# A four-layer conv/attention kernel: the MLP of layer 0 in blocks of 512 pixels, its inner units in two rounds, a chunk's products in four PSUM banks

## The chip, the cores and the metric

The kernel runs on one core of a Trainium2 chip. A core has a matrix engine (TensorE, PE in the profile; PEld is its loading of weights), two elementwise engines that can read the matrix engine's result memory PSUM (VectorE, DVE; ScalarE, ACT), GpSimd (POOL)[...], and SyncE (SP), which here only issues transfers. [...] The metric is device microseconds of the whole program, the median of several runs.

## The reference, cut to what matters

The input is 2 images of 512 channels and 32 x 32 pixels, all float32. Layer 0 is a deformable attention with a learned position bias, and then a two-layer MLP over channels; layers 1, 2 and 3 are attention layers with group norms. The change concerns the MLP and the seams on its two sides:

```
x = x + out                                   # the attention's output
xn2 = _bn(x, bn2_g, bn2_b)
h1 = gelu(einsum('bchw,oc->bohw', xn2, mlp_w1) + mlp_b1)    # 512 -> 2048 channels
x = x + einsum('bchw,oc->bohw', h1, mlp_w2) + mlp_b2        # 2048 -> 512
```

There are 2 x 1024 = 2048 pixels. Layer 1 begins with a group norm of this x, over groups of 16 channels of one image.

## The kernel before, in words

Everything is laid out with channels on the 128 partitions and pixels along the free dimension: x of an image is `xs[b]`, 4 chunks of 128 channels by 1024 pixels.

**The order of the work.** Python loops write out the order by hand. `layer0` and `layers` stand under `in_order`, so each engine runs its instructions in the order in which the code names them. Tiles and pools add the waits between engines. Loops hand small pieces of other work to the engines at given places by advancing generators (`advance`, `drain`).

**Products by seven.** A matrix product is cut in 2 x 2 blocks and done in seven block products instead of eight (the Winograd form of Strassen's scheme). `lefts` (L149) forms the four sums of the left operand, here the weights, and `rights` (L166) those of the right operand, here pixels; each sum is an operation on VectorE, and one overwrites a block of its operand. The seven products are numbered 1 to 7, and sums of them give the four blocks of the result.

**The MLP** (L1290 to L1394). `BLK = 256` pixels make a block, so a product's right operand has `PX = 128` columns. Of each block, the 2048 inner channels are made in MC = 8 steps, called chunks: a chunk gives 128 inner channels of the upper half and 128 of the lower half, for 256 pixels. `products` (L1296) allocates two banks for it, `pma` and `pmb`, and puts four products of 128 columns in the first and three in the second, in the order 1, 2, 6, 7, 5, 4, 3; each is two matmuls (512 input channels, halved, are two chunks of 128). `first_of` (L1320) copies product 1 to `p` on ScalarE; `combined` (L1306) makes the result in four additions on VectorE, `upper`, `u`, the lower half straight into `hid`, and `upper` again. `activated` applies the GELU to both halves with the bias, in two instructions on ScalarE, one chunk later; after it `form_right2` forms the right operand's sums for this chunk in `hidt`. When the eight chunks are done, layer 2 multiplies with `w2`: two halves of the output columns, seven products of eight matmuls each. It opens with product 1 of both halves, whose last matmul stands at L1382 and waits for the last GELU. `added` (L1329) adds bias and result to x and stores it to `x_d`, from which a fallback that normally does not run would start.

**What runs beside it.** Before layer 2 of a block, `normed_rights` (L180) makes the next block's normalised channels on GpSimd, four instructions, and their four sums on VectorE. In the first block `form2` makes the sums of `w2`, eight VectorE instructions of 1024 elements. From the second image on, the chunks advance `norm`, the group norm of layer 1 for the first image: statistics on VectorE, then four activations on ScalarE that write the normalised channels to the tile `hc`. In the last block the load of layer 1's weights (`qkv1`) takes the place of `w1`, after its last reader.

**Memory.** `bridge` has 8 slots of 1024 numbers per partition and outlives layer 0's pools. Layer 0 uses slots 0 to 5 (`h2p`) and 6 and 7 (part of `h2j`) in turn for sums of its bias network, early also for transposed weights (`nat`). At the end of layer 0, the sums of `w1` go to slots 0 to 5, the normalised channels to slot 6 and their sums to slot 7. `ring`, six tiles of 2048, holds the bias network's first layer; two of the six are tiles of layer 0's own pool. The tile `hc` is allocated apart, in `layers`, in the pool `chan`.

**The seam.** `finish_last` (L733) ends layer 0: it finishes the last bias sums (`third`, L651), takes the softmax of the last heads, and projects. In it `right_sums()` calls `normed_rights(0)`, after the two maximum reductions at L758, and `left_sums` forms the sums of `w1` between the last additions.

Of the kernel before, what the change touches and what calls it, by code (L numbers as in the profile page):

```python
# [12 lines left out]
F32 = mybir.dt.float32  # L13
# [66 lines left out]
def kernel(ctx: ExitStack, tc: tile.TileContext, a: dict, out: bass.AP):  # L80
# [56 lines left out]
    BLK = 256  # L137
# [42 lines left out]
    def normed_rights(blk):  # L180

        b, n = blk * BLK // HW, slice(blk * BLK % HW, blk * BLK % HW + BLK)
        xn = bridge[:, 6, :].rearrange("p (k n) -> p k n", k=CC)
        for cc in range(CC):
            nc.gpsimd.tensor_scalar(
                xn[:, cc, :], xs[b][:, cc, n], s2[:, cc : cc + 1], col("bn2_b", cc), ALU.mult, ALU.add
            )
        right, form = rights(xn, bridge[:, 7, : 3 * CC // 2 * PX].rearrange("p (i k n) -> i p k n", i=3, k=CC // 2))
        form(slice(0, CC // 2))
        return right  # L190

    def layer0(l0, fold_d, t2_b, o2_b):
# [7 lines left out]
        h2p = cycle([bridge[:, k, :] for k in range(6)])  # L200
        h2j = cycle([bridge[:, 6, :], bridge[:, 7, :], *(one.tile([P, HW], F32, name=f"h2j{k}") for k in range(2))])
# [46 lines left out]
        ring = [one.tile([P, 2 * HW], F32, name=f"h1{k}") for k in range(2)]  # L248
# [134 lines left out]
        def table(function):  # L383
            nc.scalar.activation(trial[:, 1:2], trial[:, 0:1], function)
# [348 lines left out]
        def finish_last(sim, eights, fours, right_sums, left_sums):  # L733
# [3 lines left out]
            table(AF.Exp)  # L737
            pts = [zt([P, 4, P], "pt") for _ in range(2)]
# [6 lines left out]
            project_out(pps[0], b, 0, [2])  # L745
            for n in halves:
                nc.scalar.activation(simb[:, n], sim[:, n], AF.Identity, bias=simbias[t])
# [11 lines left out]
            right_sums()  # L759
# [56 lines left out]
        nat = [bridge[:, 2 * j : 2 * j + 2, :].rearrange("p h (k n) -> p (h k) n", k=2) for j in range(3)]  # L816
# [179 lines left out]
        left1, form1 = lefts(w1s, [bridge[:, k : k + 2, :] for k in range(0, 6, 2)])  # L996
        right1 = []

        def left_sums():
# [6 lines left out]
            lambda: right1.extend(normed_rights(0)), left_sums(),  # L1006
# [195 lines left out]
    def layers(f, fold_d, t2_b, o2_b, left1, right1):  # L1202
# [5 lines left out]
        chan = f.enter_context(tc.tile_pool(name="chan", bufs=1))  # L1208
# [9 lines left out]
        def group_norm(x, gname, bname, h, small_psum):  # L1218
# [45 lines left out]
            normed = chan.tile([P, CC, HW], F32, name="hc")  # L1264
# [17 lines left out]
        with ExitStack() as mlp:  # L1282
# [8 lines left out]
            def product(pm, i, left, right, cols):  # L1291
                l, r = left[i - 1], right[i - 1]
                accumulate(pm, [(l[:, k, cols], r[:, k, :]) for k in range(l.shape[1])])

            def products(left, right, cols, some, pms=None):

                if pms is None:
                    pms = [bank(f"pm{i}").rearrange("p (j n) -> p j n", j=4) for i in "ab"]
                a, b = pms
                at = {1: a[:, 0], 2: a[:, 1], 6: a[:, 2], 3: a[:, 3], 4: b[:, 0], 5: b[:, 1], 7: b[:, 2]}  # L1300
                for i in some:
                    product(at[i], i, left, right, cols)
                return pms

            def combined(pms, p1, lower):

                a, b = pms
# [3 lines left out]
                def twice(v):  # L1311
                    return v.unsqueeze(1).to_broadcast([P, 2, PX])

                nc.vector.tensor_tensor(upper, a[:, 1:3], twice(p1), ALU.add)  # L1314
                nc.vector.tensor_tensor(u, b[:, 1:3], twice(upper[:, 1]), ALU.add)
                nc.vector.tensor_tensor(lower, b[:, 0:2], twice(u[:, 1]), ALU.add)
                nc.vector.tensor_tensor(upper[:, 1], a[:, 3], u[:, 0], ALU.add)
                return upper.rearrange("p j n -> p (j n)")

            def first_of(pms):  # L1320
                p1 = two.tile([P, PX], F32, name="p1")
                nc.scalar.copy(p1, pms[0][:, 0])  # L1322
                return p1
# [5 lines left out]
            def added(blk, m, src):  # L1329
                b, at = blk * BLK // HW, blk * BLK % HW  # L1330
                x = xs[b][:, m, at : at + BLK]
                nc.vector.scalar_tensor_tensor(x, src, col("mlp_b2", m), x, ALU.add, ALU.add)
                nc.sync.dma_start(out=x_d[b, m, :, at : at + BLK], in_=x)

# [5 lines left out]
            for blk in range(NBLK):  # L1340
                b = blk * BLK // HW
                hid = one.tile([P, HID // P, BLK], F32, name="hid")
                right2, form_right2 = rights(hid, [one.tile([P, HID // P // 2, PX], F32, name=f"hidt{i}") for i in (1, 2, 4)])

                def activated(c, upper):
                    nc.scalar.activation(hid[:, MC + c, :], hid[:, MC + c, :], AF.Gelu, bias=col("mlp_b1", MC + c))
                    nc.scalar.activation(hid[:, c, :], upper, AF.Gelu, bias=col("mlp_b1", c))

                upper = None
                for c in range(MC + 1):  # L1350
                    if c < MC:
                        pms = products(left1, right1, slice(c * P, (c + 1) * P), (1, 2, 6, 7, 5, 4, 3))
                        p1 = first_of(pms)
                    if c:
                        activated(c - 1, upper)
                    if c < MC:
                        upper = combined(pms, p1, hid[:, MC + c, :].rearrange("p (j n) -> p j n", j=2))
                    if c:
                        form_right2(slice(c - 1, c))
                    if blk == 0 and 4 <= c < MC - 1:  # L1360
                        advance(later[0])
                    if b == 1 and c % 2:
                        advance(norm)
                if blk == 0:
                    drain(chain(*later))
                    nc.vector.tensor_scalar(gb3, vb[:, 2, :], col("gamma3"), None, ALU.mult)
                if blk + 1 < NBLK:
                    right1 = normed_rights(blk + 1)
                else:
# [8 lines left out]
                both = [products(left2, right2, cols[c], ()) for c in range(2)]  # L1378
                for ks in (range(MC - 1), range(MC - 1, MC)):
                    for c in range(2):  # L1380
                        for k in ks:
                            nc.tensor.matmul(  # L1382
                                both[c][0][:, 0],
                                left2[0][:, k, cols[c]],
                                right2[0][:, k, :],
                                start=(k == 0),
                                stop=(k == MC - 1),
                            )
# [732 lines left out]
        def pixels3(x):  # L2121
            t = chan.tile([P, CC, HW], F32, name="hc")
            t = [t[:, i, :].rearrange("p (k n) -> p k n", k=2) for i in range(4)]
# [120 lines left out]
    t2_b, o2_b = [const.tile([P, CC], F32, name=name) for name in ("t2_b", "o2_b")]  # L2244
    bridge_stack = ctx.enter_context(ExitStack())
    bridge = bridge_stack.enter_context(tc.tile_pool(name="bridge", bufs=1, side="right"))
    bridge = bridge.tile([P, 8, HW], F32, name="bridge")
    with ExitStack() as l0:
        left1, right1 = layer0(l0, fold_d, t2_b, o2_b)
    with ExitStack() as fast:  # L2250
        layers(fast, fold_d, t2_b, o2_b, left1, right1)
    bad = nc.values_load(flag[0:1, 0:1], min_val=0, max_val=P)
# [88 lines left out]
```

## Time and profile before

Median of three runs: 3326.72 us (3326.65 to 3328.97).

| | |
|---|---|
| profiled execution | 3326.56 us |
| its span, first to last instruction | 3324.8 us |
| TensorE clock granted | 1.00 |
| TensorE busy | 3311.0 us |
| VectorE busy | 2643.8 us |
| ScalarE busy | 1809.0 us |
| GpSimd busy | 672.8 us |
| from 1999.6 to 2402.6 us (the MLP): TensorE busy | 402.0 us of 403.0 |
| the same stretch: VectorE busy | 214.7 us |
| the same stretch: ScalarE busy | 79.2 us |

How to read it: a row of the profile names line, engine, operation, what is written <- what is read, the shape (partitions x elements) and the count, then the busy time and the mean of one in ns, then the time that the engine sat idle just before and what ended that. Times in a timeline are us from the span's start. Instructions that run on one engine follow each other; those of different engines overlap, so only the time on the chain that ends last makes the program longer. A float32 matmul leaves two records.

### The profile page before, as it was taken

To read this page: it belongs to the slowest core of one execution; us is meant where nothing else is said; L and a number is where in the kernel's file an instruction comes from. 1 tells how busy PE (TensorE), PEld (TensorE's weight loads), DVE (VectorE), ACT (ScalarE), POOL (GpSimd) and SP (SyncE) were. 2 spreads that over 40 slices of the span, in tenths; PEclk is the share of its full clock that TensorE was granted. 3 is DMA by queue.
4 is the path that set the end of the run, shared out by engine and by line. 5 is a ranking of instruction groups with operands and counts; after the bars stand their busy time and mean duration, and the time that the engine had idled before them with its cause. 6 is when DMAs were issued, how large, how long until landed. Compare 5 with 4: busy or idle time off the path is not lost.

```text
span 3324.8 us, 60957 instructions
## 1 busy us (share of the span) xinstructions
PE 3311.0 (100%) x24805; PEld 1599.6 (48%) x24805; DVE 2643.8 (80%) x3027; ACT 1809.0 (54%) x2771; POOL 672.8 (20%) x804
## 2 busy tenths in 40 slices
PE   9999999999999999999999999999999999999999
PEld 4333333333333333333333339999953443687777
DVE  7999999999998799999999976455446466665656
ACT  4866877877876677877877642122126245122221
POOL 1333333333333233333333310000000000000000
PEclk9999999999999999999999999999999999999999
DMA  5787787787787577787787741000100100000111
GB/s 177 164 168 151 159 167 158 160 166 152 160 167 159 107 160 155 159 170 158 163 164 155 160 116 58 14 8 14 52 0 14 26 32 17 7 7 4 29 33 37
DMA packets 143121, 342.87 MB, mean 103 GB/s; under 512 B 37104, under 2 KB 52592, under 8 KB 142064
## 3 DMA queue, kind: packets, MB, share of 16 engines
q0 software_dynamic: 68112, 230.21, 37.1%
q1 hardware_dynamic: 71472, 102.12, 10.1%
q10 hardware_dynamic: 3248, 6.56, 0.5%
q8 instruction: 197, 3.23, 0.4%
q14 instruction: 92, 0.75, 0.1%
HBM read 71.46 MB, written 10.83 MB: 25 GB/s over the span
## 4 chain that ended last, share of the span: by engine, by line
PE 97%; issue 1%; ACT 1%; DVE 1%; POOL 0%; ACTq 0%; DVEq 0%; POOLq 0%
PE z L632 53%; PE pw L1479 6%; PE pma L135 6%; PE pmb L135 5%; PE pmv L1479 4%; PE score L1660 4%; PE pv L1672 3%; PE pm L1479 3%; PE score L1479 3%; PE pmt L1479 1%; PE ppr L1479 1%; PE pp L721 1%; PE sim L661 1%; PE pf L135 1%; PE pma L1382 1%
## 5 line engine op out<-in xcount | busy, mean ns | idle before, releaser
L632 PE MATMUL z<-wa,cpb_w 128*32 128x512 f32 x10880 | 1193.1, 593 | 0.5
L641 ACT ACTIVATE h<-z,b2h 128x1024 f32<-128x1024 f32 x768 | 851.2, 1113 | 327.7 <-PE z L632 316.9
L615 DVE CUSTOM_DVE_ANT_1 wa<-tab,pairs 128x2048 f32<-128x2048 f32 x340 | 779.3, 2293 | 2.7 <-PE z L632 2.4
L632 PEld LDWEIGHTS z<-wa,cpb_w 128*32 128x32 f32 x10880 | 346.1, 110 | 806.0 <-issue 713.5
L632 PE MATMUL z<-h,cpb_w 128*32 128x512 f32 x5504 | 609.4, 593 | 0.3 <-ACT h L641 0.2
L615 DVE CUSTOM_DVE_ANT_1 h<-tab,pairs 128x2048 f32<-128x2048 f32 x172 | 394.4, 2294 | 1.2 <-PE z L632 1.0
L632 PEld LDWEIGHTS z<-h,cpb_w 128*32 128x32 f32 x5504 | 175.4, 110 | 409.5 <-issue 360.1
L646 DVE SCALAR_TENSOR_TENSOR h<-h,turn,h 128x1024 f32<-128x1024 f32 x256 | 329.4, 1287 | 5.5 <-ACT h L641 5.5
L641 ACT ACTIVATE bridge<-z,b2h 128x1024 f32<-128x1024 f32 x162 | 180.6, 1115 | 118.2 <-PE z L632 118.2
L966 POOL DMA_DIRECT2D bridge<-bridge x150 | 127.5, 850 | 532.7 <-DMA bridge<-h 502.3
L646 DVE SCALAR_TENSOR_TENSOR bridge<-bridge,turn,h 128x1024 f32<-128x1024 f32 x162 | 208.1, 1285 | 3.0 <-ACT bridge L641 2.9
L974 POOL DMA_DIRECT2D bridge<-h x160 | 150.3, 939 | 287.3 <-DVE h L646 166.2
L1322 ACT COPY p<-pma 128x128 f32<-128x128 f32 x80 | 21.2, 266 | 335.7 <-PE pma L135 335.7
L1314 DVE TENSOR_TENSOR upper<-pma,p 128x256 f32<-128x256 f32 x80 | 33.8, 422 | 178.9 <-ACT p L1322 178.8
L1661 ACT ACTIVATE p<-score 128x512 f32<-128x512 f32 x256 | 129.7, 628 | 79.8 <-PE score L1660 79.4
L966 POOL DMA_DIRECT2D h2j<-h2j x90 | 76.2, 846 | 312.3 <-DMA h2j<-h 296.7
L1693 DVE TENSOR_TENSOR acc<-acc,p 128x1024 f32<-128x1024 f32 x96 | 111.4, 1219 | 28.4 <-ACT p L1661 28.4
L641 ACT ACTIVATE h2j<-z,b2h 128x1024 f32<-128x1024 f32 x94 | 104.9, 1116 | 42.7 <-PE z L632 42.7
L646 DVE SCALAR_TENSOR_TENSOR h2j<-h2j,turn,h 128x1024 f32<-128x1024 f32 x94 | 121.1, 1288 | 0.2
L1660 PE MATMUL score<-q,k 64*128 64x512 f32 x512 | 119.6, 604 | 0.0
L1672 PE MATMUL pv<-p,vT 128*64 128x512 f32 x512 | 116.5, 598 | 0.0
L979 POOL DMA_DIRECT2D bridge<-bridge x90 | 110.4, 1226 | 1.2 <-DMA bridge<-bridge 0.9
(468 smaller groups left out, 4363.2 us busy)
## 6 DMA issues: line engine op xcount, KB each, us to landing
bridge<-h POOLq DMA_DIRECT2D x160, 512.0 KB, 5.1
h2j<-h POOLq DMA_DIRECT2D x93, 512.0 KB, 5.5
bridge<-bridge POOLq DMA_DIRECT2D x159, 256.0 KB, 3.6
tab<-slog_d SPq DMA_DIRECT2D x128, 256.0 KB, 5.0
h2j<-h2j POOLq DMA_DIRECT2D x90, 256.0 KB, 3.3
bridge<-bridge POOLq DMA_DIRECT2D x150, 128.0 KB, 5.4
bridge<-bridge SPq DMA_DIRECT2D x90, 128.0 KB, 3.7
bridge<-h2j SPq DMA_DIRECT2D x90, 128.0 KB, 3.6
```

Source lines behind the costliest of these rows:

```text
L135: nc.tensor.matmul(pm, w, m, start=(k == 0), stop=(k == len(pairs) - 1))
L615: nc.vector._custom_dve(TENSOR_ADD_SAT, out=h1, in0=tx.unsqueeze(1).to_broadcast([P, H, 2, W]), in1=ty.unsqueeze(3).to_broadcast([P, H, 2, ...
L632: nc.tensor.matmul(z[point * 32 : point * 32 + 32, n], cpb_w2[:, lo : lo + 32], h1s[point][:, half * 16 : half * 16 + 16, :], start=True, ...
L641: nc.scalar.activation(h2, z, AF.Relu, bias=b2h[:, part : part + 1])
L646: nc.vector.scalar_tensor_tensor(h2, h2, turn[:, part // 2 : part // 2 + 1], parts.pop(part + 1), ALU.mult, ALU.add)
L966: nc.gpsimd.dma_start(out=own[0:P:2], in_=own[1:P:2], accum_op=ALU.add)
L974: nc.gpsimd.dma_start(out=joins[i - 1], in_=other, accum_op=ALU.add)
L1479: nc.tensor.matmul(out, stationary(l, k), moving(r, k), start=start and k == 0, stop=k == nk - 1, skip_group_check=not start,)
L1660: nc.tensor.matmul(sc, ks[m][r, s * P : (s + 1) * P], qs[m][r, n], start=True, stop=True)
L1661: nc.scalar.activation(p[:, part], sc, AF.Exp, scale=64 ** -0.5)
L1672: nc.tensor.matmul(pv[half][part * 64 : part * 64 + 64], vt[s % 4][:, lo : lo + 64], lps[s, half][:, part, :], start=(s == 0), stop=(s == 7),)
L1693: nc.vector.tensor_add(acc[half], acc[half], ps[s, half])
```

## The change

`BLK` becomes 512, so a product's right operand has 256 columns. There are 4 blocks in place of 8. So that `hid` does not grow, the inner channels are done in two rounds of RC = 4 chunks each: a round makes half of the inner channels, and its layer 2 adds their part of the output to x. The first round's part comes with the bias; the second round's is added plainly and then stored, so each pixel is stored once. `hid` and its sums are allocated once for all rounds.

A chunk's seven products of 256 columns take four banks (`slots`): 6 and 1, 4 and 5, 7 alone, 3 and 2. They run in the order 1, 6, 7, 5, 4, 2, 3. `combined` now takes the copy of product 1 in, and has six additions: five of 256 elements and one of 512. Layer 2 opens with product 1 of both halves but its last matmul, then product 2 of both halves, then that last matmul.

Normalised channels of a block (2048 numbers now) go to `h1_0`, one of `ring`'s tiles, which moves to the pool of `bridge`; their sums go to two slots of `bridge_b`. `bridge` is cut in `bridge_b` (4 slots) and `hc` (4 slots), allocated before layer 0: layer 0 uses it as slots, the sums of `w1` lie in it during the MLP, and afterwards it holds the normalised channels of the group norms and the sums of layer 3, in place of the tiles of `chan`. So the four activations that write it stand in the last round, after the last product of `w1`. In `finish_last`, the first block's normalised channels are begun at the start and their sums are formed before the maximum reductions.

```diff
-    BLK = 256
+    BLK = 512
     PX = BLK // 2
...
-        xn = bridge[:, 6, :].rearrange("p (k n) -> p k n", k=CC)
+        xn = h1_0.rearrange("p (k n) -> p k n", k=CC)
...
-        right, form = rights(xn, bridge[:, 7, : 3 * CC // 2 * PX].rearrange("p (i k n) -> i p k n", i=3, k=CC // 2))
-        form(slice(0, CC // 2))
-        return right
+        sums = bridge_b[:, 2:4, :].rearrange("p a n -> p (a n)")[:, : 3 * CC // 2 * PX]
+        right, form = rights(xn, sums.rearrange("p (i k n) -> i p k n", i=3, k=CC // 2))
+        return right, lambda: form(slice(0, CC // 2))
...
-        h2p = cycle([bridge[:, k, :] for k in range(6)])
+        h2p = cycle([*(hc[:, k, :] for k in range(4)), *(bridge_b[:, k, :] for k in range(2))])
...
-        ring = [one.tile([P, 2 * HW], F32, name=f"h1{k}") for k in range(2)]
+        ring = [h1_0, one.tile([P, 2 * HW], F32, name="h1_1")]
...
             table(AF.Exp)
+            right_sums()
...
             project_out(pps[0], b, 0, [2])
+            form_right.pop()()
...
-            right_sums()
...
-            normed = chan.tile([P, CC, HW], F32, name="hc")
+            normed = hc
...
+            def slots():
+                some = [bank(f"pm{i}").rearrange("p (j n) -> p j n", j=2) for i in "abcd"]
+                a, b, c, d = some
+                return some, {6: a[:, 0], 1: a[:, 1], 4: b[:, 0], 5: b[:, 1], 7: c[:, 0], 3: d[:, 0], 2: d[:, 1]}
+
+            def product(at, i, left, right, k0, cols, ks, nk):
                 l, r = left[i - 1], right[i - 1]
+                for k in ks:
+                    nc.tensor.matmul(at[i], l[:, k0 + k, cols], r[:, k, :], start=(k == 0), stop=(k == nk - 1))
+
+            def combined(some, at, lower):
...
+                nc.scalar.copy(p1, at[1])
+                nc.vector.tensor_tensor(upper[:, 1], at[6], p1, ALU.add)
+                nc.vector.tensor_tensor(u[:, 1], at[7], upper[:, 1], ALU.add)
+                nc.vector.tensor_tensor(u[:, 0], at[5], upper[:, 1], ALU.add)
+                nc.vector.tensor_tensor(lower, some[1], u[:, 1].unsqueeze(1).to_broadcast([P, 2, PX]), ALU.add)
+                nc.vector.tensor_tensor(upper[:, 0], at[2], p1, ALU.add)
+                nc.vector.tensor_tensor(upper[:, 1], at[3], u[:, 0], ALU.add)
...
-            def added(blk, m, src):
+            def added(blk, m, src, last):
...
-                nc.vector.scalar_tensor_tensor(x, src, col("mlp_b2", m), x, ALU.add, ALU.add)
+                if not last:
+                    nc.vector.scalar_tensor_tensor(x, src, col("mlp_b2", m), x, ALU.add, ALU.add)
+                    return
+                nc.vector.tensor_add(x, x, src)
                 nc.sync.dma_start(out=x_d[b, m, :, at : at + BLK], in_=x)
...
-            for blk in range(NBLK):
+            RC = MC // 2
+            hid = one.tile([P, 2 * RC, BLK], F32, name="hid")
+            hidt = [one.tile([P, RC, PX], F32, name=f"hidt{i}") for i in (1, 2, 4)]
+            for blk, rnd in [(blk, rnd) for blk in range(NBLK) for rnd in range(2)]:
+                last = (blk, rnd) == (NBLK - 1, 1)
+                lo = rnd * RC
...
-                for c in range(MC + 1):
+                for c in range(RC + 1):
...
+                        for i in (1, 6, 7, 5, 4, 2, 3):
+                            product(at, i, left1, right1, 0, slice((lo + c) * P, (lo + c + 1) * P), range(CC // 2), CC // 2)
...
-                    if blk == 0 and 4 <= c < MC - 1:
+                    if blk == rnd == 0 and c == 2:
                         advance(later[0])
-                    if b == 1 and c % 2:
+                    if blk == 2 and c in (1, 2, 3) or blk == 3 and c in (1, 3):
                         advance(norm)
...
+                    drain(norm)
+                elif rnd:
+                    right1, form = normed_rights(blk + 1)
+                    form()
...
+                for i, ks in ((1, range(RC - 1)), (2, range(RC)), (1, range(RC - 1, RC))):
                     for c in range(2):
+                        product(both[c][1], i, left2, right2, lo, cols[c], ks, RC)
                 for c in range(2):
-                    products(left2, right2, cols[c], (2, 6, 7, 5, 4, 3), both[c])
+                    for i in (6, 7, 5, 4, 3):
+                        product(both[c][1], i, left2, right2, lo, cols[c], range(RC), RC)
                     lower = two.tile([P, 2, PX], F32, name="lower")
-                    upper = combined(both[c], first_of(both[c]), lower)
-                    added(blk, 2 + c, lower.rearrange("p j n -> p (j n)"))
-                    added(blk, c, upper)
-        drain(norm)
+                    upper = combined(*both[c], lower)
+                    added(blk, 2 + c, lower.rearrange("p j n -> p (j n)"), rnd)
+                    added(blk, c, upper, rnd)
...
-    bridge = bridge.tile([P, 8, HW], F32, name="bridge")
+    bridge_b = bridge.tile([P, 4, HW], F32, name="bridge_b")
+    h1_0 = bridge.tile([P, 2 * HW], F32, name="h1_0")
```

More of the change, by code (lines that the diff above doesn't have):

```diff
@@ L199, in layer0 @@
         h2q = l0.enter_context(tc.tile_pool(name="att_h2q", bufs=4))
-        h2p = cycle([bridge[:, k, :] for k in range(6)])
-        h2j = cycle([bridge[:, 6, :], bridge[:, 7, :], *(one.tile([P, HW], F32, name=f"h2j{k}") for k in range(2))])
+        h2p = cycle([*(hc[:, k, :] for k in range(4)), *(bridge_b[:, k, :] for k in range(2))])
+        h2j = cycle([bridge_b[:, 2, :], bridge_b[:, 3, :], *(one.tile([P, HW], F32, name=f"h2j{k}") for k in range(2))])
         dram = l0.enter_context(tc.tile_pool(name="l0dram", bufs=1, space=DRAM))
@@ L731, in add_out, with finish_last @@
             nc.vector.scalar_tensor_tensor(x, pp[:, n], col("out_b", m), x, ALU.add, ALU.add)
-        def finish_last(sim, eights, fours, right_sums, left_sums):
+        def finish_last(sim, eights, fours, right_sums, form_right, left_sums):
             t, b, pr = NT - 1, B - 1, NPAIR - 1
@@ L814, in key_weights @@
             nc.scalar.copy(kq_w, pkw)
-        nat = [bridge[:, 2 * j : 2 * j + 2, :].rearrange("p h (k n) -> p (h k) n", k=2) for j in range(3)]
+        pairs_of = [hc[:, 0:2, :], hc[:, 2:4, :], bridge_b[:, 0:2, :]]
+        nat = [v.rearrange("p h (k n) -> p (h k) n", k=2) for v in pairs_of]
         wq, wk, wv = [lambda o, n, w=w: w[:, o, n] for w in nat]
@@ L995, in layer0, with right_sums @@
         ends = [joins.pop(steps - 4 + j) for j in range(4)]
-        left1, form1 = lefts(w1s, [bridge[:, k : k + 2, :] for k in range(0, 6, 2)])
-        right1 = []
+        left1, form1 = lefts(w1s, pairs_of)
+        right1, form_right1 = [], []
+        def right_sums():
+            right, form = normed_rights(0)
+            right1.extend(right)
+            form_right1.append(form)
         def left_sums():
@@ L1005, in layer0 @@
             sim, [joins.pop(steps - 8), joins.pop(steps - 6)], [ends[:2], ends[2:]],
-            lambda: right1.extend(normed_rights(0)), left_sums(),
+            right_sums, form_right1, left_sums(),
         )
@@ L1207, in layers @@
         keep = f.enter_context(tc.tile_pool(name="keep", bufs=1))
-        chan = f.enter_context(tc.tile_pool(name="chan", bufs=1))
         vb = keep.tile([P, 3, CC], F32, name="vb")
@@ L1290, in layers @@
             two = mlp.enter_context(tc.tile_pool(name="mlp2", bufs=2, side="right"))
-            def product(pm, i, left, right, cols):
-                l, r = left[i - 1], right[i - 1]
[L1293 to L1303, printed above, removed]
@@ L1305, in combined @@
-            def combined(pms, p1, lower):
-                a, b = pms
+            def slots():
[3 more added lines that the diff above has]
+            def product(at, i, left, right, k0, cols, ks, nk):
+                l, r = left[i - 1], right[i - 1]
+                for k in ks:
+                    nc.tensor.matmul(at[i], l[:, k0 + k, cols], r[:, k, :], start=(k == 0), stop=(k == nk - 1))
@@ L1308, in combined @@
+            def combined(some, at, lower):
                 upper = two.tile([P, 2, PX], F32, name="upper")
                 u = two.tile([P, 2, PX], F32, name="u")
[L1311 to L1316, printed above, removed]
@@ L1317, in combined @@
-                nc.vector.tensor_tensor(upper[:, 1], a[:, 3], u[:, 0], ALU.add)
+                p1 = two.tile([P, PX], F32, name="p1")
+                nc.scalar.copy(p1, at[1])
[3 more added lines that the diff above has]
+                nc.vector.tensor_tensor(lower, some[1], u[:, 1].unsqueeze(1).to_broadcast([P, 2, PX]), ALU.add)
@@ L1318, in combined @@
+                nc.vector.tensor_tensor(upper[:, 0], at[2], p1, ALU.add)
+                nc.vector.tensor_tensor(upper[:, 1], at[3], u[:, 0], ALU.add)
                 return upper.rearrange("p j n -> p (j n)")
[L1320 to L1323, printed above, removed]
             left2, form2 = lefts(
@@ L1339, in layers @@
             later = [form2(slice(c * P, (c + 1) * P)) for c in range(2)]
-            for blk in range(NBLK):
-                b = blk * BLK // HW
-                hid = one.tile([P, HID // P, BLK], F32, name="hid")
-                right2, form_right2 = rights(hid, [one.tile([P, HID // P // 2, PX], F32, name=f"hidt{i}") for i in (1, 2, 4)])
+            RC = MC // 2
+            hid = one.tile([P, 2 * RC, BLK], F32, name="hid")
+            hidt = [one.tile([P, RC, PX], F32, name=f"hidt{i}") for i in (1, 2, 4)]
@@ L1345, in activated @@
+            for blk, rnd in [(blk, rnd) for blk in range(NBLK) for rnd in range(2)]:
+                last = (blk, rnd) == (NBLK - 1, 1)
+                lo = rnd * RC
+                right2, form_right2 = rights(hid, hidt)
                 def activated(c, upper):
-                    nc.scalar.activation(hid[:, MC + c, :], hid[:, MC + c, :], AF.Gelu, bias=col("mlp_b1", MC + c))
-                    nc.scalar.activation(hid[:, c, :], upper, AF.Gelu, bias=col("mlp_b1", c))
+                    nc.scalar.activation(
+                        hid[:, RC + c, :], hid[:, RC + c, :], AF.Gelu, bias=col("mlp_b1", MC + lo + c)
+                    )
+                    nc.scalar.activation(hid[:, c, :], upper, AF.Gelu, bias=col("mlp_b1", lo + c))
@@ L1349, in layers @@
                 upper = None
-                for c in range(MC + 1):
-                    if c < MC:
-                        pms = products(left1, right1, slice(c * P, (c + 1) * P), (1, 2, 6, 7, 5, 4, 3))
-                        p1 = first_of(pms)
+                for c in range(RC + 1):
+                    if c < RC:
+                        some, at = slots()
+                        for i in (1, 6, 7, 5, 4, 2, 3):
+                            product(at, i, left1, right1, 0, slice((lo + c) * P, (lo + c + 1) * P), range(CC // 2), CC // 2)
@@ L1354, in layers @@
                     if c:
                         activated(c - 1, upper)
-                    if c < MC:
-                        upper = combined(pms, p1, hid[:, MC + c, :].rearrange("p (j n) -> p j n", j=2))
+                    if c < RC:
+                        upper = combined(some, at, hid[:, RC + c, :].rearrange("p (j n) -> p j n", j=2))
                     if c:
                         form_right2(slice(c - 1, c))
-                    if blk == 0 and 4 <= c < MC - 1:
+                    if blk == rnd == 0 and c == 2:
@@ L1361, in layers @@
                         advance(later[0])
-                    if b == 1 and c % 2:
+                    if blk == 2 and c in (1, 2, 3) or blk == 3 and c in (1, 3):
                         advance(norm)
-                if blk == 0:
+                if blk == rnd == 0:
                     drain(chain(*later))
                     nc.vector.tensor_scalar(gb3, vb[:, 2, :], col("gamma3"), None, ALU.mult)
-                if blk + 1 < NBLK:
-                    right1 = normed_rights(blk + 1)
-                else:
+                if last:
@@ L1374, in layers @@
                             nc.sync.dma_start(out=qkv1[:, k, cols], in_=a["qkv1_w"][k * P : (k + 1) * P, cols])
+                    drain(norm)
+                elif rnd:
+                    right1, form = normed_rights(blk + 1)
+                    form()
                 cols = [slice(c * P, (c + 1) * P) for c in range(2)]
-                both = [products(left2, right2, cols[c], ()) for c in range(2)]
-                for ks in (range(MC - 1), range(MC - 1, MC)):
+                both = [slots() for c in range(2)]
+                for i, ks in ((1, range(RC - 1)), (2, range(RC)), (1, range(RC - 1, RC))):
                     for c in range(2):
[L1381 to L1388, printed above, removed]
+                        product(both[c][1], i, left2, right2, lo, cols[c], ks, RC)
                 for c in range(2):
-                    products(left2, right2, cols[c], (2, 6, 7, 5, 4, 3), both[c])
+                    for i in (6, 7, 5, 4, 3):
+                        product(both[c][1], i, left2, right2, lo, cols[c], range(RC), RC)
                     lower = two.tile([P, 2, PX], F32, name="lower")
-                    upper = combined(both[c], first_of(both[c]), lower)
-                    added(blk, 2 + c, lower.rearrange("p j n -> p (j n)"))
-                    added(blk, c, upper)
-        drain(norm)
+                    upper = combined(*both[c], lower)
+                    added(blk, 2 + c, lower.rearrange("p j n -> p (j n)"), rnd)
+                    added(blk, c, upper, rnd)
         wb_stack.close()
@@ L2121, in pixels3 @@
         def pixels3(x):
-            t = chan.tile([P, CC, HW], F32, name="hc")
-            t = [t[:, i, :].rearrange("p (k n) -> p k n", k=2) for i in range(4)]
+            t = [hc[:, i, :].rearrange("p (k n) -> p k n", k=2) for i in range(4)]
             blocks = halves_of(x)
@@ L2244 @@
     t2_b, o2_b = [const.tile([P, CC], F32, name=name) for name in ("t2_b", "o2_b")]
+    hc_stack = ctx.enter_context(ExitStack())
+    hc = hc_stack.enter_context(tc.tile_pool(name="hc", bufs=1, side="right")).tile([P, CC, HW], F32, name="hc")
     bridge_stack = ctx.enter_context(ExitStack())
     bridge = bridge_stack.enter_context(tc.tile_pool(name="bridge", bufs=1, side="right"))
-    bridge = bridge.tile([P, 8, HW], F32, name="bridge")
+    bridge_b = bridge.tile([P, 4, HW], F32, name="bridge_b")
+    h1_0 = bridge.tile([P, 2 * HW], F32, name="h1_0")
     with ExitStack() as l0:
@@ L2251 @@
         layers(fast, fold_d, t2_b, o2_b, left1, right1)
+    hc_stack.close()
     bad = nc.values_load(flag[0:1, 0:1], min_val=0, max_val=P)
```

## The prediction

> **What bounds the kernel now.** I read the page's busy times and its chain of waits first, then the stage that the diff touches by stretch, by waits, by the chain in order of time, by shape, and instruction by instruction.
>
> ```profile
> PE 3311.0 (100%) x24805; PEld 1599.6 (48%) x24805; DVE 2643.8 (80%) x3027; ACT 1809.0 (54%) x2771; POOL 672.8 (20%) x804
> ...
> PE 97%; issue 1%; ACT 1%; DVE 1%; POOL 0%; ACTq 0%; DVEq 0%; POOLq 0%
> ```
> TensorE sets the end nearly everywhere. A change counts if it takes time off TensorE's stream, or makes TensorE wait. The MLP runs from its first product to layer 1's first, 1999.67 to 2402.69 in the timeline, 403.0 us:
>
> ```profile
> core 0: us, PE busy (x) PEld busy (x) DVE busy (x) ACT busy (x) POOL busy (x), PEclk, DMA share, GB/s
> 1999.60:2402.60 403.00, 402.02 (x3588) 401.35 (x3589) 214.65 (x676) 79.21 (x214) 18.70 (x28) 1.00 0.09 29
> ```
> ```profile
> PE pma L1382 <- ACT hid L1347: 0.9, 1, 0.9
> PE pma L135 <- POOL ones L1336: 0.9, 1, 0.9
> ```
> The first is the stage by stretch, the second what TensorE waited for in it: 1 us inside the stage, 0.9 us before it. VectorE is 53% busy, the clock full. So the stage is the pace of its matmuls. Its code has 8 blocks x (8 chunks x 7 products x 2 + 2 x 7 products x 8) = 1792 matmuls of 128 columns; the stretch has 3588 records, 4 of them the group norm's, so a float32 matmul leaves two. The chain in order of time (start, us, tile, records) gives the paces:
>
> ```profile
> 2033.38 5.36 PE pmb L135 x48
> ...
> 2927.17 12.09 PE pmv L1479 x56
> 2939.25 12.09 PE pw L1479 x56
> ```
> 128 columns: 5.36/24 = 0.2233 us a matmul. The other two rows are 28 matmuls of 256 columns (the view by shape lists pmv and pw as 128x256 on the same helper line): 12.09/28 = 0.4318 us, with the waits of four banks in it. Twice 0.2233 is 0.4467: a wide matmul does the work of two narrow ones in 0.0149 us less.
>
> [...]the trace's record is 5.36/48 = 111.7 ns. [...] the trace has 215.9[...]. [...]copy p reads only product 1, which runs first, and starts after the chunk's last product, which shares its bank. [...]
>
> **The change, part by part.** *(1) Matmuls.* 4 blocks x 2 rounds x (4 chunks x 7 x 2 + 2 x 7 x 4) = 896 of 256 columns. 896 x 0.4318 = 386.9 us, where 403.0 stand now: 1792 x 0.2233 = 400.1, 1.0 waited, and 1.9 over between chunks. Gain 16.1 if TensorE never waits. [...]
>
> *(2) What follows a chunk.* Four banks of eight per chunk: chunk c+2 needs chunk c's. Durations by shape, of the stage (rows out of one view):
>
> ```profile
> L1315 DVE TENSOR_TENSOR u<-pmb,upper 128x256 f32<-128x256 f32 x79 | 33.5, 424 | 2.7
> L1346 ACT ACTIVATE hid<-hid,pc 128x256 f32<-128x256 f32 x64 | 32.6, 510 | 5.8 <-DVE hid L1316 5.7
> L185 POOL TENSOR_SCALAR bridge<-x,s,pc 128x256 f32<-128x256 f32 x28 | 18.7, 678 | 310.7 <-PE pmb L135 310.2 <-POOL bridge L185 0.5
> L1224 DVE BATCH_NORM_STATS2 st<-x 128x6 f32<-128x512 f32 x8 | 5.1, 682 | 0.0
> ```
> ```profile
> 1974.26 1.29 DVE L758 TENSOR_REDUCE mx<-pt 128x8 f32<-128x512 f32 x2 [7.88 <-PE pt L757]
> ...
> 1980.14 0.69 DVE L773 TENSOR_TENSOR at<-at,sm 128x512 f32<-128x512 f32 x1
> ...
> 2023.53 1.09 POOL L185 TENSOR_SCALAR bridge<-x,s,pc 128x256 f32<-128x256 f32 x2 [24.35 <-PE pmb L135]
> ...
> 2024.86 2.42 POOL L185 TENSOR_SCALAR bridge<-x,s,pc 128x256 f32<-128x256 f32 x2 [0.24 <-POOL bridge L185]
> ```
> ```profile
> 2377.54 3.87 PE L1382 MATMUL pma<-hid,wb 128*128 128x128 f32 x32
> 2377.79 0.27 ACT L1322 COPY p<-pma 128x128 f32<-128x128 f32 x1 [2.06 <-PE pma L135]
> ```
> (The last two fences are timelines.) VectorE per chunk: five ops of 256 at 0.424, one of 512 at 0.69, four sums of 256 at 0.42: 4.5 us of a chunk's 14 x 0.4318 = 6.04. Call a chunk's end T. The last fence shows a reader starting 0.25 us after it. Only two ops then remain, because the order 1, 6, 7, 5, 4, 2, 3 and the banks (1 and 6, 5 and 4, 7, 2 and 3) let p, u and the lower half run during the chunk: T+0.25 to T+1.1. The last bank is free at T+1.1 and first written again at T+6.04+4.3. If this cover went, each us would cost 1 us per chunk, 32 in all.
>
> *(3) Layer 1 to layer 2, eight times.* Layer 2 starts with six matmuls of product 1 (2.6 us) and eight of product 2 (3.45) before the upper GELU of the last chunk is wanted, at T+6.05. That GELU ends at T+1.1 plus its own time (0.51 for 256 elements, 0.63 for an exponent of 512 in L1661; I take 0.72): T+1.9. Product 2 wants the lower GELU at T+3.9; it ends near T+0.5. The sums of the last two chunks end near T+4.6, wanted at T+6.9 by product 6. Cost nothing, spare 2.3 us. The 0.9 us wait for hid L1347, which comes from the weight sums of w2 ahead of the last chunk's ops, also goes: one of the eight such sums now runs early (c=2), seven at 1.22 us after T+4.6, and product 6 wants the next of them at T+6.9 where it ends at T+5.8.
>
> *(4) Layer 2 to the next round.* All eight banks are layer 2's. The first four were emptied under the other column half's 20 matmuls (8.6 us) and the second four are wanted 6 us into the next round. The next block's normalised channels: four POOL ops of 512 columns cost 4.4 to 9.7 us[...], then four sums of 0.69; VectorE stands behind them until T+12.6 at worst. Its next readers come at T+8.6, their banks are wanted at T+24.2, layer 2's end: hidden.
>
> *(5) Statistics, final activations, stores.* Two bn_stats and their aggregate (1.57 us) raise VectorE to 6.1 us in four chunks of the third block; the backlog of some tenths runs off in layer 2. The four hc activations (1.23 us each) all stand in the last round's layer 2, ahead of copy p on ACT, which product 6 makes due only at T+8.6. Writing hc waits for layer 1's last products, which are done. The qkv load is issued at the same event, took 10 us, and has 24.2 us instead of 25.0. Half as many stores, twice the size: nobody waits for them. Each of the sums to x goes 0.48 to 0.75 or 0.69 us, in VectorE's idle time.
>
> *(6) Layer 0 and later.* Layer 0's instructions and their waits, read from the order on each engine, are the same until its last stage; only places in memory change. There POOL starts the first block's channels (4.4 to 9.7 us, so 1972.3 at the latest[...]) when h1_0 is free (last z product, 1962.6) and VectorE forms their sums ahead of L758. The sums' places are free after the third's second half, 1971; three sums remain, to 1973.3 (1974.4 behind the slowest POOL); L758 starts at 1974.26 after 7.88 us idle. Cover 1 us, or none in the slowest case; without it the softmax starts late by what is missing, once. Later layers keep their order.
>
> **Sum.** 403.0 to 386.9, and I add 0.5 us of small waits: gain 15.6. The profiled execution took 3326.56 (span 3324.8 and 1.8 around it), so 3311.0. The median of 3326.72 lies 0.16 above, which I let go: 3311.0, with 3308.5 to 3313.5 of its own.
>
> **Rivals.** *Bubbles at the boundaries*: a wait of 0.5 to 1 us at each of 16 boundaries (8 to 2, 2 to 8) because the spare of (3) is misjudged; half the banks' depth speaks for it, the 2.3 us of spare against: 3319 to 3327, or 3315 to 3319 if it is one kind of boundary. *No gain from width*: the MLP's matmuls keep 0.2233 per 128 columns: 400.1, so 3324; pmv and pw change weights at each matmul too and run at 0.4318. *Slower*: VectorE becomes the bound in layer 1's chunks. Its price is (d - 6.04) x 32 for d us a chunk; it eats the gain at d = 6.53, and ends 0.2% slower at 6.74, half more than the 4.5 worked out. That needs wide reads of PSUM to slow beside TensorE's writes; L1315 reads PSUM beside them now[...]: 3333.4 or more.
>
> **How the numbers follow.** Differences under 0.2% (6.65 us) can't be told from no change here. Main case 0.84; boundary bubbles 0.09 (two thirds still below 3320); no gain from width 0.03; slower 0.04. Faster 0.90, same 0.06, slower 0.04. [...]
>
> **What would show it.** Right: 1792 records of 256-column matmuls near 216 ns each, the MLP at 386 to 389 us, no wait of TensorE over 1 us in it, VectorE near 4.5 us per chunk. Wrong: waits of L1306 on ACT hid (3), on DVE (2, 4), or L758 more than 12 us after the last z product, where 11.7 stand now (6).

## The result, and the profile after

The changed kernel takes 3312.09 us (median of 5 runs, 3311.18 to 3312.27), the kernel before 3326.72 (5 runs): a ratio of 0.9955 [0.9944, 0.9965], 14.6 us less. The profiled execution took 3312.27 us with a span of 3310.3, against 3326.56 and 3324.8.

The page of the changed kernel, busy times and shares of the chain of waits:

```profile
PE 3297.2 (100%) x23013; PEld 1539.6 (47%) x23013; DVE 2646.9 (80%) x2851; ACT 1799.1 (54%) x2675; POOL 665.3 (20%) x788
...
PE 98%; ACT 1%; DVE 0%; issue 0%; POOL 0%; ACTq 0%; POOLq 0%; DVEq 0%
```

TensorE still sets the end: its busy time fell by 13.8 us, while VectorE's rose by 3.1, which nobody sees. 1792 records are fewer, half of the MLP's 3584. The MLP by stretch (columns as before), and TensorE's waits from 1999 to 2390 us:

```profile
2001.00:2388.30 387.30, 387.30 (x1797) 341.01 (x1798) 216.51 (x502) 69.88 (x119) 9.10 (x12) 1.00 0.08 29
```
```profile
PE pma L1306 <- POOL ones L1336: 0.9, 1, 0.9
```

403.0 us have become 387.3, and TensorE is busy for every us of it. The one wait left is the one ahead of the stage, which the kernel before had too; the 0.9 us for hid at L1347 has gone. The chain in order of time gives the pace, here in the first layer 2:

```profile
2025.40 2.59 PE pma L1306 x12
2027.99 3.45 PE pmd L1306 x16
```

Together 6.04 us for 28 records: 215.7 ns a record, beside the 215.9 (12.09/56) that pmv and pw showed before. By shape, in the stage:

```profile
L1349 ACT ACTIVATE hid<-hid,pc 128x512 f32<-128x512 f32 x32 | 23.1, 722 | 95.8 <-DVE hid L1317 95.8
L1315 DVE TENSOR_TENSOR u<-pmc,upper 128x256 f32<-128x256 f32 x48 | 20.4, 425 | 16.1 <-PE pmc L1306 12.6
```

The GELU of 512 elements takes 0.72 us, as estimated, and VectorE's reads of PSUM take 425 ns beside wider matmuls as they took 424 beside narrow ones. A boundary from layer 1 to layer 2 (T = 2073.58 us), in a timeline:

```profile
2073.58 2.75 PE L1306 MATMUL pma<-hid,wb 128*128 128x256 f32 x12
...
2074.57 0.72 ACT L1352 ACTIVATE hid<-upper,pc 128x512 f32<-128x512 f32 x1 [0.74 <-DVE upper L1319]
...
2076.76 0.42 DVE L174 TENSOR_TENSOR hidt<-hid,hidt 128x256 f32<-128x256 f32 x1
...
2077.44 0.42 DVE L176 TENSOR_TENSOR hidt<-hid,hidt 128x256 f32<-128x256 f32 x1
...
2080.49 0.81 PE L1306 MATMUL pma<-hidt,w2s 128*128 128x256 f32 x3
```

The last upper GELU ends at T+1.7 and the last chunk's sums at T+4.3 (T+1.9 and T+4.6 were forecast); product 6 starts at T+6.9 without a wait. Last, the seam in layer 0:

```profile
1963.19 3.98 POOL L185 TENSOR_SCALAR h<-x,s,pc 128x512 f32<-128x512 f32 x4 [14.07 <-PE z L632]
...
1973.64 0.68 DVE L176 TENSOR_TENSOR bridge_b<-h,bridge_b 128x512 f32<-128x512 f32 x1
...
1975.57 1.29 DVE L760 TENSOR_REDUCE mx<-pt 128x8 f32<-128x512 f32 x2 [1.25 <-PE pt L759]
```

GpSimd needs 3.98 us, the sums end at 1974.32, and the maximum reduction still waits 1.25 us for TensorE's transposes: that is the cover.

One thing in the sum was not forecast. The MLP's gain is 15.7 us, but the MLP starts 1.3 us later (2000.99 instead of 1999.67). All of it stands already ahead of the last stage of layer 0: its first product after the bias network starts at 1963.86 instead of 1962.54, and from there to the MLP both kernels take 37.13 us. Of these 1.3 us, 0.85 come in the three warming matmuls at the start and 0.44 near 905 us, where the two programs have the same instructions.

### The profile page after: what moved, and what is told of

Same layout as the page of the kernel before. It is cut to its first block, busy times and chain, and to the rows that moved or that the text cites. A ratio compares the mean times of both kernels' runs of the same rounds, so it can differ in the third digit from the quotient of the medians.

```text
span 3310.3 us, 56995 instructions
## 1 busy us (share of the span) xinstructions
PE 3297.2 (100%) x23013; PEld 1539.6 (47%) x23013; DVE 2646.9 (80%) x2851; ACT 1799.1 (54%) x2675; POOL 665.3 (20%) x788
## 4 chain that ended last, share of the span: by engine, by line
PE 98%; ACT 1%; DVE 0%; issue 0%; POOL 0%; ACTq 0%; POOLq 0%; DVEq 0%
PE z L632 53%; PE pw L1480 6%; PE pmv L1480 4%; PE score L1661 4%; PE pv L1673 3%; PE pma L1306 3%; PE pmd L1306 3%; PE pmb L1306 3%; PE pm L1480 3%; PE score L1480 3%; PE pmc L1306 2%; PE pp L721 2%; PE pmt L1480 1%; PE ppr L1480 1%; PE sim L661 1%; PE pf L135 1%
## 5 line engine op out<-in xcount | busy, mean ns | idle before, releaser
L968 POOL DMA_DIRECT2D bridge_b<-bridge_b x110 | 93.3, 848 | 379.0 <-DMA bridge_b<-h 369.6
L641 ACT ACTIVATE bridge_b<-z,b2h 128x1024 f32<-128x1024 f32 x116 | 129.3, 1114 | 67.4 <-PE z L632 66.2
L646 DVE SCALAR_TENSOR_TENSOR bridge_b<-bridge_b,turn,h 128x1024 f32<-128x1024 f32 x116 | 148.5, 1280 | 1.0 <-ACT bridge_b L641 0.9
L976 POOL DMA_DIRECT2D bridge_b<-h x115 | 110.3, 959 | 124.9 <-DVE h L646 86.1
L1313 ACT COPY p<-pma 128x256 f32<-128x256 f32 x48 | 17.9, 372 | 200.5 <-PE pma L1306 200.4
L976 POOL DMA_DIRECT2D h2j<-h x93 | 92.6, 996 | 52.0 <-DVE h L646 42.0
L1480 PE MATMUL pmv<-wa,hc 128*128 128x256 f32 x384 | 89.5, 380 | 0.1
```

The source lines that it names most:

```text
L641: nc.scalar.activation(h2, z, AF.Relu, bias=b2h[:, part : part + 1])
L646: nc.vector.scalar_tensor_tensor(h2, h2, turn[:, part // 2 : part // 2 + 1], parts.pop(part + 1), ALU.mult, ALU.add)
L968: nc.gpsimd.dma_start(out=own[0:P:2], in_=own[1:P:2], accum_op=ALU.add)
L976: nc.gpsimd.dma_start(out=joins[i - 1], in_=other, accum_op=ALU.add)
L1480: nc.tensor.matmul(out, stationary(l, k), moving(r, k), start=start and k == 0, stop=k == nk - 1, skip_group_check=not start,)
```

## The experiments

In the timeline the MLP, from its first product to layer 1's first, took 403.0 us before and 387.3 after. Times below stand beside 3312.09; the kernel before had medians of 3326.59, 3326.73 and 3326.94 beside them.

### Narrow matmuls again

```diff
+                whole = nk > CC // 2 and i == 1
+                for h in [slice(0, PX)] if whole else [slice(0, PX // 2), slice(PX // 2, PX)]:
-                for k in ks:
+                    for k in ks:
-                    nc.tensor.matmul(at[i], l[:, k0 + k, cols], r[:, k, :], start=(k == 0), stop=(k == nk - 1))
+                        nc.tensor.matmul(
+                            at[i][:, h], l[:, k0 + k, cols], r[:, k, h], start=(k == 0), stop=(k == nk - 1)
+                        )
```

> The changed kernel, with 832 of its 896 matmuls of 256 columns cut into two of 128 (the 64 of product 1 in layer 2 stay whole). Banks, rounds, chunks and order stay. Theory[...]: 832 x (2 x 0.2233 - 0.4318) = 12.4 us back, the MLP at 399.8 instead of 387.4, the time near 3324.5. Rival (the gain came from half as many chunks and from waits that went): the MLP within 1 us of 387.4, the time near 3312.

3323.72 us (3323.13 to 3325.19, 12 runs), 11.6 longer. The MLP by stretch, and two pieces of its chain:

```profile
2000.00:2399.80 399.80, 399.80 (x3461) 396.50 (x3462) 217.02 (x502) 69.91 (x119) 9.86 (x12) 1.00 0.08 29
```
```profile
2043.00 1.79 PE pmc L1308 x16
2044.78 3.57 PE pmb L1308 x32
```

3.57/32 = 111.6 ns a record is the old pace, and the MLP takes 399.8 us, the number worked out. With rounds, banks and order kept, 12.5 of the 15.7 us went back: they are the width. The 64 matmuls left whole would hold another 64 x 0.0149 = 1.0, an estimate from the two paces of the trace before. The rest, 2.2 us, fits what the kernel before spent outside its pace of 0.2233 (the 0.9 us wait, and ends of chunks; 2.9 us before, 0.4 after); no run separates it. The rival without width falls, but for this rest.

The run nearly doubles the weight loads (PEld, the second pair in the rows by stretch) together with the matmuls: they are busy for 396.5 of 399.8 us here, and for 341.0 of 387.3 us in the changed kernel. So it doesn't tell whether the 0.0149 us belong to the matmul itself or to the weight loads beside it; that stays open.

### Layer 2 opens with product 1 whole

```diff
-                for i, ks in ((1, range(RC - 1)), (2, range(RC)), (1, range(RC - 1, RC))):
+                for i, ks in ((1, range(RC)), (2, range(RC))):
```

> The changed kernel, but layer 2 of each round opens with product 1 whole, without product 2 ahead of its last matmul. The upper GELU of the last chunk ended 1.7 us after layer 2's start (T) and is now wanted at T+1.3 (three matmuls of 0.4318) instead of T+6.05. Theory: a wait of some 0.45 us in each of 8 rounds, 3.6 us in all, near 3315.7. If the GELU is not what a boundary hangs on: no change. If the boundary has more behind it than that GELU: over 1 us a round, 8 us or more.

3315.53 us (3314.61 to 3315.96, 6 runs), 3.4 longer; the MLP 391.4, 4.1 longer, or 0.5 a round. TensorE's waits in the MLP:

```profile
PE pma L1306 <- ACT hid L1352: 1.8, 6, 0.3
```

The profile now names the upper GELU at six of the eight boundaries, with 0.3 us each. Counted by the starts it is more, as at the second one, in a timeline:

```profile
2073.28 1.46 PE L1306 MATMUL pma<-hid,wb 128*128 128x256 f32 x6
2075.04 2.42 PE L1306 MATMUL pma<-hid,wb 128*128 128x256 f32 x10 [0.31 <-ACT hid L1352]
```

From start to start it is 1.76 us, where the pace gives 6 x 0.2159 = 1.30: TensorE loses 0.46 us, the 0.45 expected. The idle time is counted from a matmul's modelled end, which lies 0.16 us later than that. Over eight rounds this makes 3.7 of the 4.1 us. So a boundary hangs on that GELU, and product 2 ahead of it is worth 4 us. This is the rival of bubbles at the boundaries, brought about by the order; with the order of the change it didn't come.

### Every bank read after the chunk

```diff
-                        for i in (1, 6, 7, 5, 4, 2, 3):
+                        for i in (5, 4, 7, 2, 3, 6, 1):
```

> The changed kernel with each chunk's products of layer 1 in the order 5, 4, 7, 2, 3, 6, 1, so that every reader of the banks waits for the chunk's last product. The readers then end near T+3.5 instead of T+1.1. Theory (depth of banks is the cover, the order gives it little): the last bank is free at T+3.5 and first written again near T+10; the upper GELU ends T+4.3 (wanted T+6.05), the sums T+6.7 (wanted T+6.9): 0 to 2 us longer in all. Rival (the order is the cover): 2.4 us in each of 32 chunks, 75 us; or in each of 8 boundaries only, 10 to 20 us.

3311.23 us (3311.0 to 3312.07, 4 runs): no change that the median can tell. The MLP takes 387.8 us, 0.5 longer. TensorE's waits from 1998 to 2388 us:

```profile
PE pmb L1306 <- DVE x L731: 0.8, 1, 0.8
PE pma L1306 <- DVE w2s L161: 0.2, 1, 0.2
```

The first is the wait ahead of the stage, under another name. At the first boundary copy p starts 0.26 us after T and the last reader ends at T+3.1 instead of T+1.0; TensorE waits 0.2 us for it, once, where the first round's sums of w2 stand behind it. The depth of four banks (a bank is one of the eight tiles of 512 float32 numbers in the kernel's pool `banks`) is the cover; the order within a chunk is worth 0.5 us at most.

### More work for VectorE in each chunk

```diff
                         upper = combined(some, at, hid[:, RC + c, :].rearrange("p (j n) -> p j n", j=2))
+                        for _ in range(n):
+                            nc.vector.tensor_tensor(spare, spare, spare, ALU.add)
```

`spare` is a tile of 128x512, zeroed once at the start, that nothing else reads; n is 2, 4 and 5.

> The changed kernel with two idle sums of 128x512 (0.69 us each, on a tile of their own) on VectorE behind each of the 32 chunks' combinations. VectorE's work per chunk goes from 4.5 to 5.9 us, below a chunk's 6.04. Theory (a spare of 1.5 us per chunk, 2.3 us at the boundary): no change but for the four chunks with statistics and the first round's weight sums, 0 to 3 us. Rival (VectorE is near its bound, through reads of PSUM beside TensorE's writes): 10 us or more.

> Four such sums instead of two: VectorE's work per chunk is 7.26 us, over 6.04. By the price in the prediction's slower rival, (7.26 - 6.04) x 32 = 39 us longer, near 3351. Rival: four banks of depth and the 24 us of layer 2 absorb the backlog of a round, so TensorE waits only where layer 2 wants the last chunks' sums (3 x 1.2 us late against a spare of 2.3, or less): 1.5 to 3.5 us in each of 8 rounds, 12 to 28 us longer.

Two: 3311.16 us (3310.47 to 3312.27, 4 runs) and an MLP of 387.3, no change. So there are 1.4 us of slack per chunk, and VectorE's bound is not near. Four: 3327.24 us (3325.45 to 3330.88, 12 runs), 15.2 longer, the MLP 403.2. TensorE's waits in it, and three stretches of 2 us behind the 3.2 us wait:

```profile
PE pma L1306 <- DVE hidt L174: 3.8, 2, 2.0
PE pma L1306 <- DVE w2s L161: 3.2, 1, 3.2
PE pg L1236 <- DVE mean L1243: 2.7, 1, 2.7
PE pmd L1306 <- ACT hid L1351: 1.1, 1, 1.1
```
```profile
2034.00:2036.00 2.00, 2.00 (x5) 1.63 (x6) 2.00 (x2) 0.00 (x0) 0.00 (x0) 0.51 0.00 0
2036.00:2038.00 2.00, 2.00 (x7) 1.57 (x7) 1.97 (x3) 0.30 (x1) 0.00 (x0) 0.64 0.00 0
2038.00:2040.00 2.00, 2.00 (x11) 1.77 (x10) 2.00 (x3) 0.08 (x1) 0.00 (x0) 1.00 0.00 0
```

Neither expectation was right in its detail. The price per chunk would have been 39 us. The depth does absorb a round's backlog, and better than I expected: from 2050 to 2200 us TensorE is busy for all 150 us, so the three rounds there, in which VectorE has no other work (plain rounds), cost nothing. The waits listed, 10.8 us in all, fall in rounds where it has other work, the sums of w2 and the group norm. And the clock (third column from the end) falls to 0.51 and 0.64 behind the 3.2 us wait and to 0.50 behind the 2.0 us wait of the last round: 1.7 us lost each time. Waits and clock make 14.2 of the 15.9 us. Five times the 0.16 us that the profile's idle time leaves out are another 0.8; where the last 0.9 are I have not found. Since plain rounds just held at four, I asked what a fifth sum does.

> Five idle sums of 0.71 us behind each chunk's combinations: VectorE's work per chunk is some 8.0 us. With four, rounds without other work on VectorE hid all of it: in the round at 2077 us the last sums that product 6 reads ended at T+8.19, and its fourth matmul of the first column half wanted them at T+8.2, so nothing was left there. Theory (the boundary's spare is 4.6 us, counted to that matmul, and is used up at four): the fifth makes each of 8 rounds wait 4 x 0.71 = 2.9 us more, and a wait of 2 to 3.2 us twice cost some 1.7 us of lower clock behind it: 23 us (clock never lost) to 37 us (lost each time) more than with four, 3350 to 3364. Rival (a price per chunk once over 6.04 us): (7.98 - 6.04) x 32 = 62 us over 3312, near 3374. Rival (more depth still): 5 us more than with four, near 3332.

3346.43 us (3345.93 to 3347.1, 4 runs), 19.2 longer than with four; the MLP 422.8. Two of the waits in plain rounds:

```profile
2085.13 2.43 PE L1306 MATMUL pmd<-hid,wb 128*128 128x256 f32 x10 [1.58 <-ACT hid L1351]
...
2140.57 0.70 PE L1306 MATMUL pma<-hidt,w2s 128*128 128x256 f32 x2 [0.76 <-DVE hidt L174]
```

Now every round waits, also for the lower GELU, but a plain round by 0.8 to 2.4 us, not by 2.9: the size was too high by about a third. The price per chunk (62 us) and more depth (5 us) both fall. The threshold is where it was reckoned, four to five sums.

### GpSimd three times as long at the seam

```diff
-        for cc in range(CC):
+        for cc in [*range(CC)] * (3 if blk == 0 else 1):
```

> The changed kernel with the four GpSimd operations for the first block's channels done three times over (the same values). They took 3.98 us from 1963.2, so now end near 1975.1, and VectorE's four sums of 0.69 near 1977.9 instead of 1974.3, ahead of the max reduction, which started at 1975.57. Theory (a cover of 1.25 us, then the softmax is late once): 2.4 to 3.1 us longer. Rival (the softmax's end has slack of its own under TensorE's projections): 0 to 0.5 us.

3311.97 us (3311.69 to 3312.1, 4 runs), within the scatter; the profile tells it. The seam in a timeline:

```profile
1962.21 11.37 POOL L185 TENSOR_SCALAR h<-x,s,pc 128x512 f32<-128x512 f32 x12 [14.07 <-PE z L632]
...
1975.43 1.28 DVE L760 TENSOR_REDUCE mx<-pt 128x8 f32<-128x512 f32 x2
```

Layer 0's last stage starts 0.97 us earlier here, so with the old cover L760 would start at 1974.60. It starts 0.83 us later, straight behind the sums, and from the last stage's first product to the MLP it is 37.95 us instead of 37.13: 0.82. TensorE's wait for the softmax grew from 0.5 to 1.4 us. So what the sums are late, the MLP starts late, once, as the prediction had it. My 2.4 to 3.1 was wrong in size: GpSimd ended 0.6 us sooner than three times 3.98, and the first of the four sums ran before its end, at 1971.67 us, not behind it.

### The sums back behind the maximum reductions

```diff
             table(AF.Exp)
-            right_sums()
...
-            form_right.pop()()
...
                 nc.vector.tensor_reduce(mx[:, g], ptvs[half], AX.X, ALU.max, negate=True)
+            right_sums()
+            form_right.pop()()
```

> The changed kernel with the sums of the first block's channels put back behind the two max reductions, where they stood before the change. Theory: 2.75 us of sums from 1976.9 to 1979.65, where the reciprocal started at 1978.87, so the softmax ends 0.8 us later, and TensorE, which waited 0.5 us for it, 0.8 us more: the stretch from layer 0's last z product to the MLP's first product goes from 37.1 to 37.9 us. Rival (that place is hidden too): 37.1.

3310.99 us (3310.94 to 3311.8, 3 runs), no difference that the median can tell. The waits show it: TensorE waits for the softmax's first half 1.0 us instead of 0.5,

```profile
PE pt L779 <- DVE at L774: 1.0, 1, 1.0
```

but the second half of the softmax is not later for it, and the stretch to the MLP is 37.43 us instead of 37.13 (37.09 to 37.14 in all profiles but the two of the seam). The new place of the sums is worth 0.3 us, not 0.8.

### The kernel before, once more

> The kernel before, profiled once more. The changed kernel's layer 0 lay 1.3 us later, of which 0.85 us stand already in the three warming matmuls at the start (5.31 against 4.46 us) and 0.44 us near 905 us. Theory (both differ from run to run, whatever the kernel): the profiles of this and of the other runs show warming matmuls of both lengths. Rival (it belongs to the changed kernel's program): 4.4 to 4.5 us here, and near 5.3 us in every run made from the changed kernel. The MLP takes 403.0 us in both cases.

3326.69 us (3326.0 to 3328.12, 10 runs), the MLP 403.0 again. The first product of layer 0's last stage, in timelines of the kernel before, of its second profile, and of the run with two idle sums:

```profile
1962.54 3.70 PE L721 MATMUL pp<-aT,vo 128*128 128x512 f32 x8
```
```profile
1964.04 3.70 PE L721 MATMUL pp<-aT,vo 128*128 128x512 f32 x8
```
```profile
1962.24 3.70 PE L721 MATMUL pp<-aT,vo 128*128 128x512 f32 x8
```

The same program got there 1.5 us later the second time, and programs with the changed kernel's layer 0 (eight other profiles) got there between 1962.24 and 1962.98, all sooner than the changed kernel's own 1963.86. So the 1.3 us are scatter of layer 0, not a cost of the change. The warming matmuls took 4.46 and 4.27 us in the two profiles of the kernel before and 4.51 to 5.49 in the others: the rival's 5.3 in every such run falls, though a small difference between the programs isn't excluded; layer 0's length doesn't follow them. What makes them differ from run to run, no run shows. What the 0.44 us near 905 us are stays open, but they don't belong to the program: from the first record of L661 at 903 us to that of L504 it takes 7.42 us in the changed kernel's profile and 6.98 in the kernel before's. In the chain of waits, from L661's piece to L504's, it is 7.31 and 6.86 us in these two, 7.45 in the run with product 1 whole, and 6.86 or 6.87 in the runs with narrow matmuls, two and four idle sums, late reads, and the sums back.

## Why the prediction was right

*(1) Matmuls*: 386.9 us worked out, 387.3 measured, and the two records of a matmul at 215.7 ns. The pace of a shape, read from another stage of the same trace, held here, to 0.4 us. So the size of the gain is right and shown to be the width's, but what inside a matmul saves it isn't shown. The range around the sum, 3308.5 to 3313.5, was the author's estimate. The narrow run gave back 12.5 us, where the widths of its 832 matmuls account for 12.4.

*(2) VectorE per chunk*: 4.5 of 6.04 us was right, and the slack of 1.4 us was shown. Its last sentence was wrong if it means the early reads: had they gone, each us would have cost 1 us a chunk. They went in one run and it cost 0.5 us in all, because the last bank is wanted again only near T+10. The depth itself no run took away.

*(3) Layer 1 to layer 2*: no wait, as said, and the opening order, by which the GELU isn't wanted before T+6.05, was needed: without it 0.5 us a round. The spare of the sums, 2.3 us, was mis-sized. It was counted to the last of the four sums and to product 6's first matmul. But product 6 reads the second sum (t2), which ends at T+3.6, and the last chunk's part only in its fourth matmul, 1.3 us later, at T+8.2: the spare is 4.6 us. That is why plain rounds bore four idle sums.

*(4), (5)*: nothing waited there in the changed kernel; no run took their cover away alone.

*(6) Layer 0*: a cover of 1 us was forecast, 1.25 measured; the four GpSimd operations took 3.98 us, below the range of 4.4 to 9.7, an estimate at four times 1.09 and 2.42 us, what two pairs of narrower ones took.

*The sum*: 15.6 forecast, 15.7 in the MLP, and 14.6 between the medians; the profiled execution lost 1.3 us in layer 0. The 0.5 us added for small waits came as 0.4 us over the pace, without a wait. The runs with two idle sums and with late reads lie 15.4 and 15.5 us below the medians of the kernel before taken beside them. Scatter of layer 0 had no place in the sum, though the three runs known of before already lay 2.3 us apart.

*The rivals*: no gain from width is refuted, boundary bubbles were absent. The slower one had the wrong price. It multiplied the excess over 6.04 us by 32 chunks and put its break-even at 6.53 us of VectorE's work per chunk. The run with 7.3 us (four idle sums at the 0.71 us that they took) needed 3327.24 us, 0.65 more than the kernel before beside it, so break-even is there: the excess of a round gathers over four chunks, spends the boundary's 4.6 us first, and runs off during layer 2. The idle sums stand in for slow reads of PSUM here; no run has reads that are slow themselves.

## What to carry to other kernels

Where TensorE is busy for every us of a stage, look for a stage of the same kernel that runs the wider shape: its pace per matmul, times the count, gave this stage's time to within 0.4 us. Before pricing a slower helper engine per step, ask how many steps its backlog may gather before TensorE reads the result, and count to the instruction that reads it, not to the first of its group. A gain of some us is best checked inside its stage, since layer 0 alone moved by 1.8 us between profiles.

## What the runs showed of the hardware

- A wait of TensorE can cost more than its length. Behind all three waits of over 3 us (3.2, 3.6, 4.2) in the runs with four and five idle sums, and behind two of 2.0 and 2.4 us, the granted clock fell to about 0.5 for 3 to 7 us; three of 2.2, 2.6 and 2.7 us left it at 1.00. So the length of a wait alone did not decide it: 2.0 us were enough once, and 2.7 us were not.
- VectorE took longer where GpSimd's channels ran beside it. The last addition of the bias sums took 1.68 us in the changed kernel's profile and in those of the two seam runs, in which they do (L996), and 1.23 us in the kernel before's, in which they don't (L994):

```profile
1966.56 1.68 DVE L996 TENSOR_TENSOR bridge_b<-bridge_b,h 128x1024 f32<-128x1024 f32 x1
```
```profile
1965.15 1.23 DVE L994 TENSOR_TENSOR bridge<-bridge,h 128x1024 f32<-128x1024 f32 x1
```

  Its tile lies elsewhere in memory, which these two don't separate. But the first sum of 512 at L173 took 0.69 us behind GpSimd's end, and 1.27 us beside it, in the run with GpSimd three times as long, on the same tile. GpSimd's four operations took 3.98 us beside the 1.68 us addition, and two of them 1.52 us at 2073.48 us.
